# A transformer layer on one core: softmax sums divided through memory, bfloat16 transposes of the maxima, and filler products on TensorE

## The chip, the cores and the metric

One core of one Trainium2 chip runs the whole layer in one launch. The metric is the device time of one execution in microseconds; the median of several runs is compared. The engines are TensorE (PE, with its weight loads, PEld), VectorE (DVE), ScalarE (ACT), GpSimd (POOL) and SyncE (SP, which here only issues DMAs).

## The reference

The input x is 2 batches x 2048 tokens x 256 channels, float32. The layer is

```python
x = x + attention(layernorm(x))      # 16 heads of 16 channels, rotary q and k, causal
x = x + ffn(layernorm(x))            # 256 -> 704 -> 256, fp4-rounded inputs and weights
# attention, per head:
att = softmax(where(causal, q @ k.T / 4, -inf))
y = att @ v;  return y @ Wo.T + bo
# ffn:
h = silu(fp4(x) @ fp4(w_gate).T) * (fp4(x) @ fp4(w_up).T);  return fp4(h) @ fp4(w_down).T
```

fp4 rounds blocks of 16 channels to eight magnitudes after scaling by the block's largest value, so that earlier results must be nearly exact in float32.

## The kernel before

The tokens are cut into 8 chunks (b, c) of 512, four for each batch, and the 16 heads into 4 groups g of four. A pair (chunk, group) is a slot; there are 32. Work on a slot falls into four steps.

- **Maxima** (`max_steps`): for 128 queries at a time, TensorE computes scores with queries on partitions (line 1020, tile `sc`, two heads at once in two 64-row strips, causal mask added by line 988), and DVE reduces each 512-wide bank to a maximum (line 1044).
- **Turning the maxima**: DVE splits each maximum into three summands that fit bfloat16 (lines 1082 and 1085) and puts them into `mslots`, a float32 tile of 128 queries x 4 x (4 heads x 32 places). Four float32 transposes on TensorE (line 1098, tile `ptm`) put the queries on the free axis, and ACT casts them to the bfloat16 tile `mT` (line 1104).
- **Values** (`value_steps`): scores come again with keys on partitions (line 1158, tile `sx`), after a bfloat16 product that subtracts the maxima (line 1150, `less` x `mT`). ACT takes the exponential (line 1173), and TensorE multiplies by v (line 1206, tile `av`). v has a column of ones ahead of each head's 16 channels, so `av` holds for each head, in 32 partitions, one row of sums and 16 rows of unnormalised values, 512 queries wide. ACT copies it to `avs` (line 1228).
- **Dividing** (`divide`): four float32 transposes on TensorE (line 1240, tile `pty`) put queries back on partitions; DVE takes the reciprocal of the sums (line 1250) and multiplies (line 1254) into `y`, queries x channels.

When all four groups of a chunk are divided, `ffn_steps` runs for each of its four 128-token tiles: `y` is transposed once more, two float32 transposes (line 1296, `pth<-ident,y`) and an ACT copy to `yT` (line 1300, in the buffers `xT`), because the output product `po` (line 1380) needs channels on partitions; then come layernorm, fp4 rounding (mostly on POOL), the gate and up products `pg` (line 1430), their gating, rounding, and the down product `pd` (line 1523). Projections of the next chunk (`pj`, line 763, `pv`, line 945) run among them; their rotated q and k go to DRAM (`parts`, line 855) and come back in the strip layout (`qT`, line 866, and `kT`, line 879), all on SP's queue.

**What sets the order.** Every piece of work is a task with an engine, a cost in microseconds, a due time and the things it reads and writes. `Plan.ordered` simulates the engines with these costs, picks the task that can start first (among those within `PATIENCE` of the first, the one due earliest), gives buffers out as `ROOM` allows, and the instructions are emitted in that order. For the engines in `ORDERED` (PE, DVE, ACT, POOL) each instruction is chained to the one before it, so that the order stays; SP's DMAs are not chained, and may be moved ahead by the scheduler below. All engines run their instructions in order: an instruction that waits holds up those behind it.

The due times come from the slots: slot n's maxima, then slot n's values during slot n+1, the division after that (`divided`), and the FFN of a chunk spread over the slots after its last division. The last chunk's FFN has nothing to run beside, and uses its own due times and buffers (`last`).

Of the kernel before, what the change touches and what calls it, by code (L numbers as in the profile page):

```python
# [34 lines left out]
ALU = mybir.AluOpType  # L35
# [21 lines left out]
    mybir.EngineType.DVE,  # L57
    mybir.EngineType.Activation,
    mybir.EngineType.Pool,
)  # L60
MAGIC = 1.5 * 2.0**22
EXPONENT = 0x7F800000
# [5 lines left out]
CHANGE = 0.07  # L68
FEED_M = 0.0
FEED_V = 0.0  # L70
PATIENCE = 0.03
TURN = 0.4
ISSUE = 0.46

ON_VECTOR = (0, 1, 2, 3)
LAST = 0.05
# [6 lines left out]


XIN = 3
ROOM = dict(ps=7, av=1, ex=4, qT=5, parts=4)
ROOM.update(mx=2, mparts=1, left=1, mT=2, avs=1, den=2, y=2)
ROOM.update(xnT=1, xin=XIN, high=1, t1=1, t2=1, cs=1, dev=XIN-1)
ROOM.update(x0=1, xT=2, x1=2, xn=2, h=1, hrT=1, step=1, fdev=2, sc16=2, sc44=2)


ANY_TURN = ("ps",)
# [25 lines left out]


class Task:  # L120
    __slots__ = "engine cost run due tiling late left ready end after new kinds".split()


class Plan:
# [47 lines left out]
    def ordered(self):  # L172

        waiting = {e: [] for e in HOP}
        for n, t in enumerate(self.tasks):
            if not t.left:
                waiting[t.engine].append((t.due, n, t))
        number = {t: n for n, t in enumerate(self.tasks)}
        free = dict.fromkeys(HOP, 0.0)
        rooms = {kind: [] for kind in ROOM}  # L180
        turn = dict.fromkeys(ROOM, 0)
        tiling = "whole"
        dues = sorted(((t.due, n) for n, t in enumerate(self.tasks)), reverse=True)
        done = set()
        out = []

        def vacancy(kind, n, to):

            held = rooms[kind]
            n -= ROOM[kind] - len(held)  # L190
            if n <= 0:
                return 0.0, []
            some = []
            for thing in held:
                if all(u.end is not None for u in thing.users):
                    at = max(
                        u.end + (u.late if u.engine != SP else 0.0) + HOP[u.engine][to]
                        for u in thing.users
                    )
                    some.append((at, thing.number, thing))  # L200
            if len(some) < n:
                return None
            some = sorted(some)[:n]
            return some[-1][0], [thing for *_, thing in some]

        while len(out) < len(self.tasks):
            while dues and dues[-1][1] in done:
                dues.pop()
            horizon = dues[-1][0] + AHEAD
            choice = None  # L210
            for e, queue in waiting.items():
                queue.sort(key=lambda x: x[:2])
                able = []
                vacant = {}
                for due, n, t in queue:
                    if due > horizon or len(able) > 30:
                        break
                    at = max(t.ready, free[e])
                    for kind, some in t.kinds.items():
# [24 lines left out]
            e = t.engine  # L244
            waiting[e].remove((due, n, t))
            for kind, some in t.kinds.items():
                for thing in vacancy(kind, len(some), e)[1]:
                    rooms[kind].remove(thing)
                rooms[kind] += some
                turn[kind] += len(some)  # L250
            if e == PE:
                if t.tiling != tiling:
                    at += ENTER[t.tiling]
                tiling = t.tiling
            if e == SP:
# [12 lines left out]
        self.span = max(t.end for t in out)  # L268
        return out
# [29 lines left out]
def layer_kernel(  # L299
# [28 lines left out]


    const = ctx.enter_context(tc.tile_pool(name="const", bufs=1))  # L330
    qry = ctx.enter_context(tc.tile_pool(name="qry", bufs=5))
    spill = ctx.enter_context(
        tc.tile_pool(name="spill", bufs=4, space=bass.MemoryType.DRAM)
    )
# [52 lines left out]
        less.append(t)  # L387
    minus_half = const.tile([P, 1], F32, name="minus_half")
    nc.gpsimd.memset(minus_half, -0.5)
    mslots = const.tile([P, TPC, GROUP, SLOT], F32, name="mslots")  # L390
    nc.gpsimd.memset(mslots, 0.0)

# [592 lines left out]
    def masked(sc, h, col, mask):  # L985
        for half in range(2):
# [6 lines left out]
                stop=(half == 1),  # L993
            )

    maxima, max_ = {}, {}

    m_order, e_order = Thing(), Thing()
# [3 lines left out]
    def max_steps(b, c, g):  # L1002
# [89 lines left out]
        def turn(due):  # L1092
            pm = Thing("ps")

            def run():
                st["pt"] = small(CH, "ptm").rearrange("p (i q) -> p i q", i=TPC)
                for i in range(TPC):
                    nc.tensor.transpose(
                        st["pt"][:, i, :], mslots[:, i].rearrange("p s d -> p (s d)"), ident
                    )  # L1100

            def put():
                mT = att.tile([P, CH], BF16, tag="mT", name="mT")
                nc.scalar.copy(mT, st["pt"].rearrange("p i q -> p (i q)"))
                maxima[b, c, g] = mT

            add(
                PE,
                turning(TPC),
                run,  # L1110
                [slots_of, fixed],
                [pm],
                due - 0.1,
                [max_[b, c, g]],
                late=0.05,
            )
            add(ACT, on_scalar(CH), put, [pm], [max_[b, c, g]], due - 0.1)
# [5 lines left out]
        return steps, split, turn  # L1123

    rows, rows_ = {}, {}

    def value_steps(b, c, g):

# [96 lines left out]
        def close(due):  # L1225
# [3 lines left out]

            add(ACT, on_scalar(CH), run, [av_], [avs_], due)  # L1230

        def divide(due):
            pm = Thing("ps")
            if g == 0:
                rows_[b, c] = Thing("y")
# [80 lines left out]
    def ffn_steps(b, c, i, last=False):  # L1316
# [40 lines left out]
        def turn_attended(due):  # L1357
            def put():
# [8 lines left out]
                [things["x0"]],  # L1367
                due,
            )
            transposed(  # L1370
                lambda: rows[b, c][:, i, :], E, rows_[b, c], put, things["yT"], due
            )

        def attended(due):
            pm = Thing("ps")

            def run():
                po = st["po"] = small(E, "po")
# [10 lines left out]
                token("x1")  # L1389
                nc.vector.tensor_tensor(st["x1"], st["po"], st["x0"], ALU.add)  # L1390

            add(PE, KE * product(E), run, [things["yT"], wo_], [pm], due, [things["x1"]])
# [170 lines left out]
        ]  # L1563


    order = [(b, c) for b in range(B) for c in range(NC)]
    slots = NG * len(order)

    def placed(steps, lo, hi):
# [100 lines left out]
    for n in range(4):  # L1670

        to = spread[:, n, :].rearrange("p (h half x e) -> p h half x e", h=2, half=2, x=2)
        for twice in range(2):
            dst = to[:, :, twice, n % 2, :] if n < 2 else to[:, :, n % 2, twice, :]
            nc.vector.tensor_copy(dst, fold.rearrange("p (h e) -> p h e", h=2))
    begun = [(-10.0 + 0.01 * n, step) for n, (_, step) in enumerate(norm_steps(*order[0]))]
    steps = [step for _, step in project_steps(*order[0], 0)]
    raws = {}
# [113 lines left out]
```

## Time and profile before

| | |
|---|---|
| runs | 1398.01, 1398.54, 1400.73 us; median 1398.54 |
| profiled execution | 1400.22 us; its span, first to last instruction, is 1398.2 us |
| mean granted TensorE clock | 0.976 |
| DMA | 69.22 MB, mean 50 GB/s |
| SP | 426 DMA issues, 186.4 us of issuing |

The profile lists for each engine its busy time, then the same in 40 slices of 35 us as tenths. A group of instructions is shown as line, engine, operation, output<-inputs, shape and count, busy time and the mean ns of one, and then the idle time of its engine just before it with what ended that idle time. The matrix products in float32 stand as two records each; the transposes as one. The granted clock (PEclk) is the share of its full rate that TensorE was given.

### The profile page before, as it was taken

Reading aid. Unit: us, or ns where it says so; the run is one execution under the profiler, and the core shown is the slowest. Engines: PE = TensorE matmul, PEld = TensorE weight load, DVE = VectorE, ACT = ScalarE, POOL = GpSimd, SP = SyncE. Lnnn points to the kernel's source line nnn. Section 1 sums busy time; section 2 is a strip of 40 time slices with the busy share of each in tenths; the row PEclk is TensorE's granted clock in tenths of the full one; section 3 lists DMA queues with packets and bytes.
Section 4 is the critical chain, followed back from the end, with each engine's and each line's share of the span. In section 5 each row is a group of like instructions: output and inputs, shape, how many; then the busy total and the mean of one; then the engine's idle time right before and its main releaser. Section 6 shows DMA issues by size and latency. Waiting matters only on the chain. (4 is left out here: it accounts for less than half of the span.)

```text
span 1398.2 us, 27614 instructions
## 1 busy us (share of the span) xinstructions
PE 1338.2 (96%) x10437; PEld 675.2 (48%) x10437; DVE 1117.2 (80%) x2442; ACT 759.6 (54%) x1698; POOL 520.7 (37%) x671
## 2 busy tenths in 40 slices
PE   6898999999999999999999999999999999999986
PEld 3454445544544444444465455455454444444454
DVE  6779989988889988875477978998888988983286
ACT  2533665466556556567743455455655556667711
POOL 4655634434413433224353543242442331320342
PEclk9887999999999999999999999999999999999998
DMA  2443424202111301020422404130120120000000
GB/s 91 116 108 80 90 67 93 54 16 61 35 24 53 65 24 41 16 53 25 95 66 53 125 25 90 50 69 12 54 54 5 53 56 11 9 8 9 5 5 15
DMA packets 46316, 69.22 MB, mean 50 GB/s; under 512 B 6372, under 2 KB 22120, under 8 KB 46184
## 3 DMA queue, kind: packets, MB, share of 16 engines
q1 hardware_dynamic: 45888, 67.20, 20.4%
q8 instruction: 82, 1.34, 0.4%
q14 instruction: 50, 0.41, 0.1%
q10 hardware_dynamic: 296, 0.26, 0.1%
HBM read 47.52 MB, written 19.92 MB: 48 GB/s over the span
## 5 line engine op out<-in xcount | busy, mean ns | idle before, releaser
L1173 ACT ACTIVATE ex<-sx 128x512 f32<-128x512 f32 (+3 forms) x1280 | 594.0, 538 | 358.4 <-PE sx L1158 201.5
L1044 DVE TENSOR_REDUCE parts<-sc 128x1 f32<-128x512 f32 (+3 forms) x1152 | 638.9, 612 | 64.0 <-PE sc L1020 41.2
L1158 PE MATMUL sx<-qT,kT 64*128 64x512 f32 (+3 forms) x1280 | 339.2, 521 | 0.0
L1206 PE MATMUL av<-ex,v 128*32 128x512 f32 (+3 forms) x2560 | 300.6, 540 | 0.2 <-ACT ex L1173 0.2
L1020 PE MATMUL sc<-kT,qT 64*128 64x512 f32 (+3 forms) x1280 | 291.2, 430 | 9.1 <-DVE parts L1044 1.9
L1150 PE MATMUL sx<-mT,less 64*128 64x512 bf16 (+3 forms) x1280 | 249.5, 355 | 4.7 <-DVE mx L1044 2.0
L1020 PEld LDWEIGHTS sc<-kT,qT 64*128 64x128 f32 x1280 | 138.5, 190 | 156.9 <-DVE parts L1044 46.8
L517 POOL TENSOR_SCALAR inv<-inv 128x16 f32<-128x16 f32 (+2 forms) x82 | 18.0, 220 | 509.7 <-DVE inv L513 472.0
L1150 PEld LDWEIGHTS <-less 64*128 64x128 bf16 x1280 | 68.6, 94 | 211.1 <-issue 203.5
L1158 PEld LDWEIGHTS sx<-qT,kT 64*128 64x128 f32 x1280 | 132.6, 195 | 8.9 <-issue 6.5
L1523 PE MATMUL pd<-wdT,hrT 128*128 128x256 f32 (+1 forms) x384 | 103.6, 410 | 0.7 <-ACT hrT L1300 0.3
L1206 PEld LDWEIGHTS av<-ex,v 128*32 128x32 f32 x2560 | 52.0, 108 | 74.2 <-issue 65.9
L1523 PEld LDWEIGHTS pd<-wdT,hrT 128*128 128x128 f32 (+1 forms) x384 | 70.0, 197 | 29.8 <-issue 15.6
L1430 PE MATMUL pg<-wgT,xT 128*128 128x352 f32 x224 | 77.1, 478 | 1.0 <-ACT qb L776 0.3
L1044 DVE TENSOR_REDUCE mx<-sc 128x1 f32<-128x128 f32 (+3 forms) x128 | 54.6, 479 | 25.8 <-PE sc L988 25.6
L1430 PE MATMUL pg<-wuT,xT 128*128 128x352 f32 x224 | 74.3, 472 | 0.2
L763 PE MATMUL pj<-xnT,wqkT 128*128 128x512 f32 x128 | 73.3, 671 | 1.1 <-DVE v L954 0.6
L542 POOL TENSOR_TENSOR h<-h,step 128x704 f32<-128x704 f32 x28 | 47.2, 1686 | 68.6 <-DVE step L539 66.9
L988 PE MATMUL sc<-pick,mask_q 64*128 64x64 bf16 x1024 | 70.9, 201 | 0.0
L1456 ACT ACTIVATE h<-pg 128x352 f32<-128x352 f32 x64 | 30.0, 469 | 69.2 <-PE pg L1430 59.6
L815 POOL TENSOR_TENSOR t<-t,cs 128x512 f32<-128x512 f32 x31 | 39.6, 1279 | 75.1 <-DVE t L809 70.5
L988 PE MATMUL sx<-pick,mask_k 64*128 64x64 bf16 x1024 | 64.1, 196 | 0.0
(153 smaller groups left out, 1592.1 us busy)
## 6 DMA issues: line engine op xcount, KB each, us to landing
qT<-parts SPq DMA_DIRECT2D x120, 128.0 KB
kT<-parts SPq DMA_DIRECT2D x120, 128.0 KB
parts<-high SPq DMA_DIRECT2D x30, 256.0 KB
parts<-t SPq DMA_DIRECT2D x30, 256.0 KB
cs<-in_rope_dram SPq DMA_DIRECT2D x8, 512.0 KB
xin<-in_L_attn_x_dram SPq DMA_DIRECT2D x28, 128.0 KB
x<-in_L_attn_x_dram SPq DMA_DIRECT2D x28, 128.0 KB
out_dram<-x SPq DMA_DIRECT2D x28, 128.0 KB
```

The lines of the kernel that those rows point to most:

```text
L542: queue.tensor_tensor(src(), src(), st["step"], ALU.add)
L763: nc.tensor.matmul(got["pj"], lhsT=wqkT[:, k, i, cols], rhs=xnTs[b, c][:, k, :], start=(k == 0), stop=(k == KE - 1),)
L815: (nc.gpsimd if early and i == 0 else queue).tensor_tensor(swapped, swapped, angles[b, c][:, 1, :], ALU.mult)
L988: nc.tensor.matmul(sc[h][:, col + at : col + at + STRIP], lhsT=strips(mask, h, half), rhs=strips(pick, h), start=False, stop=(half == 1),)
L1020: nc.tensor.matmul(sc[h][:, :cols], lhsT=strips(qT, h, d, slice(i * P, (i + 1) * P)), rhs=strips(kT, h, duo, slice(0, cols)), start=True, ...
L1044: nc.vector.tensor_reduce(dst, got[0][h][:, :cols], AX.X, ALU.max)
L1150: nc.tensor.matmul(sc[h][:, off:], lhsT=strips(less[d], h), rhs=strips(mT, h, slice(off, CH)), start=True, stop=False,)
L1158: nc.tensor.matmul(sc[h][:, off:], lhsT=strips(kT, h, duo, slice(jj, jj + P)), rhs=strips(qT, h, d, slice(off, CH)), start=False, stop=(j ...
L1173: nc.scalar.activation(st[j, d][:, h, off:], got[0][h][:, off:], AF.Exp, scale=HD**-0.5)
L1206: nc.tensor.matmul(st["av"][SLOT * s : SLOT * (s + 1), off:], lhsT=v[:, at : at + SLOT], rhs=st[j, d][:, h, off:], start=(j == 0), stop=(j ...
L1430: nc.tensor.matmul(got[half], lhsT=split("xrT")[:, k, :], rhs=wT[:, k, half * IH : (half + 1) * IH], start=(k == 0), stop=(k == KE - 1),)
L1523: nc.tensor.matmul(st["pd"], lhsT=st["hrT"][:n, k, :], rhs=wdT[:n, k, :], start=(k == 0), stop=(k == KI - 1),)
```

## The change

1. **Division** (all chunks but the last; the last keeps the old path). `laid_apart` writes `avs` to DRAM (`sums`), reads the 4 x 512 sums back as a 128 x 16 tile (`den`), takes the reciprocal there on DVE, writes it to DRAM, and reads it back with each row repeated over 16 partitions (`over`). The 64 rows of values are read from DRAM into `y`, which now has channels on partitions. After each second group POOL multiplies 128 x 512 by `over`. There are five DMAs for each group. `po` takes `y` directly as its stationary operand; the transpose to `yT` and its copy go.
2. **Maxima**: the four transposes of line 1098 read the upper halves of `mslots` as bfloat16, with a bfloat16 identity, into a bfloat16 bank.
3. **Filler products**: between a task due at -999 and one due at 12 (`KEPT`), `keep` puts products of the identity with its first 64 columns, whose result nothing reads, into TensorE's order ahead of each task whose planned idle time is over 0.1 us, one for each 0.12 us. In the built program there are 268, of which 46 stand ahead of the first projection.
4. **Order and buffers**: SP joins `ORDERED`; `PATIENCE` goes from 0.03 to 0.06; the `qT` buffers go from 5 to 4 and `xT` from 2 to 1.

```diff
+    mybir.EngineType.SP,
...
-PATIENCE = 0.03
+PATIENCE = 0.06
...
+KEPT = 12.0
+SPARED = 0.1
...
-ROOM = dict(ps=7, av=1, ex=4, qT=5, parts=4)
-ROOM.update(mx=2, mparts=1, left=1, mT=2, avs=1, den=2, y=2)
+ROOM = dict(ps=7, av=1, ex=4, qT=4, parts=4)
+ROOM.update(mx=2, mparts=1, left=1, mT=2, avs=1, den=2, y=2, sums=2, over=1)
...
-ROOM.update(x0=1, xT=2, x1=2, xn=2, h=1, hrT=1, step=1, fdev=2, sc16=2, sc44=2)
+ROOM.update(x0=1, xT=1, x1=2, xn=2, h=1, hrT=1, step=1, fdev=2, sc16=2, sc44=2)
...
             def run():
-                st["pt"] = small(CH, "ptm").rearrange("p (i q) -> p i q", i=TPC)
+                upper = mslots.bitcast(BF16).rearrange("p i s (d two) -> p i (s d) two", two=2)
+                bank = ps_s.tile([P, TPC, P], BF16, tag="ps", name="ptm")
+                st["pt"] = bank
                 for i in range(TPC):
-                    nc.tensor.transpose(
-                        st["pt"][:, i, :], mslots[:, i].rearrange("p s d -> p (s d)"), ident
-                    )
+                    nc.tensor.transpose(st["pt"][:, i, :], upper[:, i, :, 1], ident_b)
...
-                turning(TPC),
+                0.01 + 0.08 * TPC,
...
+        def laid_apart(due):
...
+            def out():
+                st["sums"] = spill.tile([P + GROUP, CH], F32, tag="sums", name="sums", bufs=2)
+                nc.sync.dma_start(st["sums"][:P], st["avs"])
+            def dens():
+                st["den"] = att.tile([P, HD], F32, tag="den", name="den")
+                nc.sync.dma_start(
+                    st["den"], inner()[:, 0, :].rearrange("s (n e) -> s n e", e=HD)
+                )
+            def over_out():
+                nc.sync.dma_start(
+                    st["sums"][P:].rearrange("s (n e) -> s n e", e=HD), st["den"]
+                )
+            def sums():
...
+                nc.sync.dma_start(rows[b, c][at, g // 2, :], inner()[:, 1:AUG, :])
+            def over_in():
...
+                nc.sync.dma_start(
+                    overs[b, c][at],
+                    st["sums"][P:].unsqueeze(1).to_broadcast([GROUP, HD, CH]),
+                )
+            def times():
+                y = rows[b, c][:, g // 2, :]
+                nc.gpsimd.tensor_tensor(y, y, overs[b, c], ALU.mult)
+            add(SP, landing(256), out, [avs_], [sums_], due)
+            add(SP, landing(8) , dens, [sums_], [den_], due)
+            add(SP, landing(128), sums, [sums_], [y_part], due, [rows_[b, c]])
+            add(DVE, 0.25, lambda: nc.vector.reciprocal(st["den"], st["den"]), [], [den_], due)
+            add(SP, landing(8), over_out, [den_], [sums_], due)
+            add(SP, landing(128), over_in, [sums_], [over_part], due, [over])
...
+            if g % 2:
...
+                add(POOL, on_pool(CH), times, [*over.parts, *pair], [*pair, rows_[b, c]], due)
         def divide(due):
+            if (b, c) != order[-1]:
+                return laid_apart(due)
...
-            transposed(
-                lambda: rows[b, c][:, i, :], E, rows_[b, c], put, things["yT"], due
-            )
+            if last:
+                transposed(
+                    lambda: rows[b, c][:, i, :], E, rows_[b, c], put, things["yT"], due
+                )
...
-                        lhsT=split("yT")[:, k, :],
+                        lhsT=(
+                            split("yT")[:, k, :]
+                            if last
+                            else rows[b, c][:, k, i * P : (i + 1) * P]
+                        ),
...
+    def keep(n=1):
+        if not kept:
+            kept.append(small(P, "kept"))
+        for _ in range(n):
+            nc.tensor.matmul(
+                kept[0][:, :STRIP], lhsT=ident, rhs=ident[:, :STRIP], start=True, stop=True
+            )
+    add(PE, 0.3, keep, [fixed], [held], -999.0)
+    add(PE, 0.3, keep, [held], [], KEPT)
...
     for t in plan.ordered():
+        if t.engine == PE and held.users[0].end <= t.start <= held.users[-1].end:
+            keep(max(0, int((t.idle - SPARED) / 0.12)))
         t.run()
```

More of the change, by code (lines that the diff above doesn't have):

```diff
@@ L120 @@
 class Task:
-    __slots__ = "engine cost run due tiling late left ready end after new kinds".split()
+    __slots__ = "engine cost run due tiling late left ready end after new kinds start idle".split()
 class Plan:
@@ L254, in ordered @@
                 tiling = t.tiling
+                t.start, t.idle = at, at - free[e]
             if e == SP:
@@ L330, in layer_kernel @@
     const = ctx.enter_context(tc.tile_pool(name="const", bufs=1))
-    qry = ctx.enter_context(tc.tile_pool(name="qry", bufs=5))
+    qry = ctx.enter_context(tc.tile_pool(name="qry", bufs=4))
     spill = ctx.enter_context(
@@ L389, in layer_kernel @@
     nc.gpsimd.memset(minus_half, -0.5)
+    ident_b = const.tile([P, P], BF16, name="ident_b")
+    nc.vector.tensor_copy(ident_b, ident)
     mslots = const.tile([P, TPC, GROUP, SLOT], F32, name="mslots")
@@ L994, in masked @@
             )
+    order = [(b, c) for b in range(B) for c in range(NC)]
     maxima, max_ = {}, {}
@@ L1125, in layer_kernel @@
     rows, rows_ = {}, {}
+    overs, over_ = {}, {}
     def value_steps(b, c, g):
@@ L1230, in close, with inner @@
             add(ACT, on_scalar(CH), run, [av_], [avs_], due)
+        def laid_apart(due):
+            if g == 0:
+                rows_[b, c] = Thing("y")
+            if g % 2 == 0:
+                over_[b, c, g] = Thing("over")
+            over = over_[b, c, g - g % 2]
+            wide = GROUP * HD
+            at = slice(g % 2 * wide, g % 2 * wide + wide)
+            sums_, den_ = Thing("sums"), Thing("den")
+            y_part, over_part = Thing(of=rows_[b, c]), Thing(of=over)
+            rows_[b, c].parts = getattr(rows_[b, c], "parts", []) + [y_part]
+            def out():
+                st["sums"] = spill.tile([P + GROUP, CH], F32, tag="sums", name="sums", bufs=2)
+                nc.sync.dma_start(st["sums"][:P], st["avs"])
+            def inner():
+                return st["sums"][:P].rearrange("(s r) q -> s r q", s=GROUP)
+            def dens():
[8 more added lines that the diff above has]
+            def sums():
+                if g == 0:
+                    rows[b, c] = att.tile([P, KE, CH], F32, tag="y", name="y")
+                nc.sync.dma_start(rows[b, c][at, g // 2, :], inner()[:, 1:AUG, :])
+            def over_in():
+                if g % 2 == 0:
+                    overs[b, c] = att.tile([P, CH], F32, tag="over", name="over", bufs=1)
+                nc.sync.dma_start(
[11 more added lines that the diff above has]
+            add(SP, landing(128), over_in, [sums_], [over_part], due, [over])
+            over.parts = getattr(over, "parts", []) + [over_part]
+            if g % 2:
+                pair = rows_[b, c].parts[-2:]
+                add(POOL, on_pool(CH), times, [*over.parts, *pair], [*pair, rows_[b, c]], due)
@@ L1390, in put @@
                 nc.vector.tensor_tensor(st["x1"], st["po"], st["x0"], ALU.add)
-            add(PE, KE * product(E), run, [things["yT"], wo_], [pm], due, [things["x1"]])
+            turned = things["yT"] if last else rows_[b, c]
+            add(PE, KE * product(E), run, [turned, wo_], [pm], due, [things["x1"]])
             add(DVE, on_vector(E), put, [pm, things["x0"]], [things["x1"]], due)
@@ L1563, in ffn_steps @@
         ]
-    order = [(b, c) for b in range(B) for c in range(NC)]
     slots = NG * len(order)
@@ L1675, in layer_kernel @@
             nc.vector.tensor_copy(dst, fold.rearrange("p (h e) -> p h e", h=2))
+    held = Thing("ps")
+    kept = []
+    def keep(n=1):
[7 more added lines that the diff above has]
+    add(PE, 0.3, keep, [held], [], KEPT)
     begun = [(-10.0 + 0.01 * n, step) for n, (_, step) in enumerate(norm_steps(*order[0]))]
```

## The prediction, made before the changed kernel ran

> **What bounds the kernel now.** I read the busy times first, then the 40 slices, then the busy times by stage, and last the order of time around one removed transpose.
>
> ```profile
> PE 1338.2 (96%) x10437; PEld 675.2 (48%) x10437; DVE 1117.2 (80%) x2442; ACT 759.6 (54%) x1698; POOL 520.7 (37%) x671
> PE   6898999999999999999999999999999999999986
> DVE  6779989988889988875477978998888988983286
> PEclk9887999999999999999999999999999999999998
> ```
>
> PE is busy nearly throughout; only the first five slices (to 175 us) and the last two show gaps. The granted clock is low in just these places. A busy PE could still be a waiting PE, since ends are modelled. So I took the distance from the start of each group of products to the start of the next, between 175 and 1330 us: 214 value products of 512 columns take 0.996 us at the 10th and 0.999 at the 90th percentile, and with every group put at the median of its kind the sum is 97% of the time that passed. PE runs at its own rate there, and what leaves it there comes off the time.
>
> ```profile
> core 0: us, PE busy (x) PEld busy (x) DVE busy (x) ACT busy (x) POOL busy (x), PEclk, DMA share, GB/s
> 29.20:39.50 10.30, 10.02 (x54) 5.11 (x56) 8.44 (x25) 2.90 (x6) 3.73 (x7) 0.50 0.01 2
> 42.90:49.70 6.80, 5.81 (x44) 3.94 (x44) 6.59 (x23) 3.51 (x7) 4.41 (x8) 0.50 0.27 77
> 80.40:94.10 13.70, 13.41 (x84) 7.36 (x82) 11.55 (x33) 2.23 (x5) 4.94 (x7) 0.50 0.40 112
> 124.80:141.90 17.10, 14.05 (x64) 8.00 (x62) 16.69 (x45) 3.87 (x8) 7.59 (x12) 0.50 0.11 29
> 175.00:1330.00 1155.00, 1138.15 (x9128) 560.87 (x9121) 925.22 (x1978) 677.62 (x1496) 400.89 (x473) 1.00 0.19 45
> ```
>
> The first four rows are the stretches between 29 and 142 us where the clock is a half. DVE is busy for 43.3 of their 47.9 us. In the last row PE idles for 16.9 us and DVE is busy for 80%.
>
> **Division, on TensorE.** The next view gives the price.
>
> ```profile
> 860.96 0.59 PE L1158 MATMUL sx<-qT,kT 64*128 64x512 f32 x2
> 861.49 0.66 PE L1240 MATMUL pty<-ident,avs 128*128 128x128 f32 x4
> 861.98 0.38 PE L1296 MATMUL pth<-ident,y 128*128 128x128 f32 x2
> 862.20 1.02 PE L763 MATMUL pj<-xnT,wqkT 128*128 128x512 f32 x2
> ```
>
> The columns are start, length over all, and the group. From start to next start the four transposes of `avs` hold PE for 0.49 us (mean of the 27 such groups after 175 us: 0.517), the two of `y` for 0.22 here (mean of 28: 0.43, since others wait for the shape to change). Seven of eight chunks leave both: 28 groups x 0.517 = **14.5 us**, and 28 tiles x 0.43 = **12.0 us**. The way in counts too: from the score product at 860.96 to the transposes are 0.53 us, where one score pair follows another after 0.457 (median). 56 insertions x 0.07 = 4 us; with zero and twice that as ends I take **4**.
>
> **Division, elsewhere.** These rows leave with them.
>
> ```profile
> L1250 DVE RECIPROCAL den<-pty 128x16 f32<-128x16 f32 x32 | 7.8, 245 | 7.8 <-PE pty L1240 7.8
> L1254 DVE TENSOR_TENSOR y<-pty,den 128x256 f32<-128x256 f32 x32 | 13.6, 425 | 1.1
> L1300 ACT COPY xT<-pth 128x256 f32<-128x256 f32 x56 | 21.2, 388 | 10.1 <-PE pth L1296 10.0
> ```
>
> DVE loses 28 x 0.425 = 11.9 us (the reciprocal stays, on the same 128x16), ACT 28 x 0.388 = 10.9. POOL gains 14 products of 128x512 at 1.279 (row `t<-t,cs`), 17.9 us on an engine busy for 37%. Hidden behind PE, all of it, and counted at nothing; without that cover POOL's 1.28 would stand once in each chunk's chain.
>
> SP gains 140 issues: 28 x (0.58 for 256 KB, as `parts`, and 4 x 0.35, as the loads of x) = 55 us on 186 of issuing. It also waits, and what it waits for shows in its own waits:
>
> ```profile
> SPq L866 <- DMA parts<-t: 46.8, 14, 4.2
> SPq L879 <- DMA parts<-t: 18.8, 14, 2.6
> ```
>
> Total, times, longest. A trip to DRAM and back makes SP wait 1.3 to 3.3 us on average, 4.2 at most. The chain from `avs` to a divided `y` is 0.59 (copy), 2.0 of issues, four landings of 2.1 to 4.2, 0.25 (reciprocal) and 1.28 (POOL): 12 to 21 us in place of some 1.3. Behind its waiting DMAs in SP's queue stand q and k for later slots, x for the FFN, and stores. The chain costs PE something only if `po` comes up in PE's order before it is done. In the changed program's order, priced with the distances above, PE has 16 to 48 us of other work between the last value product of each of the seven chunks and its first `po`. The shortest, 16, belongs to chunk (0, 3). So one chunk may wait up to 5 us: I take **+2**, with 0 and 5 x 7 = 35 as ends.
>
> **Maxima.** 32 groups of four float32 transposes become bfloat16. No bfloat16 transpose is in the trace. The float32 one has a start-to-start of 109 ns; the upper bound is no gain. For bfloat16 the subtraction product (line 1150) averages 388 ns at 512 columns and 223 at 128: 0.43 ns a column, 55 ns for 128. 4 x 54 x 32 = **6.9 us** off; the ends are 0 and 14 (all of it, 32 x 0.44). I take 6.9, since the per-column rate is a bfloat16 row's own. If the two-byte reads at a stride of four bytes cost extra, the gain shrinks towards nothing.
>
> **Filler products and the clock.** 268 products of 64 columns in float32, two records each. A float32 record of 352 columns has a start-to-start of 296 ns (gate products), so 64 columns make 54 ns, and one filler 0.108: 29 us in all at full clock, twice that at half. PE idled 27 us before 175 us. Laid into waits the fillers cost nothing, laid over work 29. Their purpose can only be the clock. Had the half-rate stretches run at full rate, PE's 43.3 busy us there would be 21.6 less, but DVE, busy for 43.3 of the 47.9, would leave 4.6. I take **-5** for the clock (ends 0 and -21.6) and **+2** for fillers that miss a wait (ends 0 and 29).
>
> Here the trace and a rule part. In the half-rate stretches PE is busy for 43.3 of 47.9 us, and its longest wait between 20 and 175 us is this, after the last of them:
>
> ```profile
> PE ptm L1098 <- DVE x L1390: 2.5, 1, 2.5
> ```
>
> The Trainium skill, page "TensorE: Matmul & The Clock Gate", section "What's actually happening", has the clock fall to a half after an idle window of about 3.4 us. No such idle window is in that row, so the trace does not bear the rule out as it stands; something weaker than full idleness was enough. By the rule the fillers would cure nothing and the clock term would be 0, the time 5 us higher.
>
> **Order and buffers.** `PATIENCE` reshuffles the order: it can win at most the 16.9 us that PE idles after 175 us, and lose as much by the same measure; I take 0. One `qT` buffer less lets q for the next slots come later; zero in the sum, and a rival below. One `xT` less goes with `yT`, its second user. SP's chaining takes away early starts such as the x loads, which wait in SP's queue for up to 35.7 us (SP's waits, line 1353), so nothing is lost.
>
> **The sum**, on the profiled execution's 1400.22 us (span 1398.2 and 2.0 around it): -14.5 - 12.0 - 4 - 6.9 - 5 + 2 + 2 = -38.4, so 1361.8. The median of the runs shown is 1.7 lower than that execution; against it **1360 us**. Next bound: still PE after 175 us, with DVE at (925 - 12) of about 1120, 82%.
>
> **Rivals.**
>
> - *The clock comes back whole, and waits close too.* If DVE's load in the half-rate stretches moves under other work, the clock gives 21.6 rather than 5: 1360 - 16.6 = **1343**. For it: DVE has 22 us of idle time between 29 and 175 us. Against: in each stretch it is DVE that is nearly full.
> - *DVE becomes the bound.* DVE releases the banks of `sc`. In slices such as 910 to 945 it is busy for 34.3 of 35 us. If it sets the pace wherever PE is relieved, only its own loss counts, 11.9 us, with part of the clock: about **1383**. Against: the medians at 97%.
> - *Slower: q comes late.* With four `qT` buffers, the second pair of a block can be loaded only after an earlier slot's values are done, and in SP's queue it stands behind the division's landings; 9 of 15 block loads are split in two in the changed order. `sc` and `sx` of a slot stand at the head of PE's order and hold everything. It decides from 38 us over 28 slots: 1.4 us a slot. At 2 us, less than one landing, it gives 1360 + 56 = **1416**. For it: the waits on landings average 1.3 us and more. Against: slots last 13 to 71 us (from one turning of maxima to the next), and a buffer frees a slot ahead of its use.
> - *The change does not do what it says*: the clock stays at a half in the same places and fillers fall on work, +29 and the 5 lost: 1360 + 32 = **1392**, still within reach of the removed transposes.
>
> **How the numbers follow.** The sum 0.53, the whole clock 0.14, DVE 0.15, no use of the fillers 0.08 (half of it within 0.2% of before, which is 2.8 us and about what a measurement of this kernel can tell from no change), late q 0.10. Faster: 0.53 + 0.14 + 0.15 + 0.04 = 0.86; same 0.04; slower 0.10. The unknowns of the first case (transposes 0 to 14, way in 0 to 8, chain 0 to 35, PATIENCE) spread it by some 15 each way. The range runs from below the whole clock's 1343 to past DVE's 1383: 1336 to 1388, leaving out 0.18 above and a little below.
>
> **What would show it.** Right: `ptm` distances near 55 ns; no `pty` or `pth<-ident,y` before the last chunk; the stage from 175 us to the tail shorter by about 33 us with PE as busy; the clock at full from 20 to 175 us with at most 5 us won. Wrong: idle PE ahead of `po` released by POOL (the chain), ahead of `sc` or `sx` released by a DMA into `qT` (late q), bank waits on DVE in the steady stage, or half-rate stretches in the same places.

## The result and the profile after

| | before | after |
|---|---|---|
| median of 6 runs, us | 1399.08 | 1445.61 |
| lowest to highest | 1398.01 to 1402.88 | 1435.44 to 1457.19 |
| granted clock, by run | 0.976 (profiled) | 0.959 to 0.976 |

The change makes the kernel slower: ratio 1.0318, 95% interval 1.0275 to 1.036. I had said 1360 us. The profiled execution of after is its slowest run (1457.19 us, clock 0.959, so that its profile overstates the clock losses); it is not counted in the ratio, and where a time of after is compared below, it is the median of the other five, 1442.58 us. These five go from 1451.4 us at a granted clock of 0.966 to 1435.4 at 0.976, 16 us for 0.010 of the clock.

The same rows of the page, now of after: busy times, then the slices of PE, DVE and the clock.

```profile
PE 1403.8 (96%) x10805; PEld 734.7 (50%) x10805; DVE 1112.7 (76%) x2415; ACT 751.1 (52%) x1670; POOL 537.8 (37%) x685
...
PE   9999999999999999999998999999999999999986
...
DVE  5457698897888888888448978898888978894276
...
PEclk9589899999999999999999999999999999999998
```

PE is fuller than before in the first five slices and DVE emptier. The clock is low in the second slice, in the midst of filler products. From the costliest groups, the fillers and their weight loads:

```profile
L1760 PE MATMUL kept<-ident 128*128 128x64 f32 x536 | 89.6, 327 | 1.3 <-POOL ident masks.py:199 1.3
L1760 PEld LDWEIGHTS kept<-ident 128*128 128x128 f32 x536 | 82.9, 238 | 7.3 <-issue 4.3
```

They are busy for 90 us, where I had reckoned 29. The stages of after (start:end, length, busy us of PE, PEld, DVE, ACT and POOL with counts, clock, DMA share, GB/s):

```profile
32.00:73.00 41.00, 40.48 (x210) 29.06 (x210) 22.38 (x61) 8.03 (x17) 12.62 (x21) 0.50 0.17 43
175.00:1330.00 1155.00, 1128.61 (x8932) 554.33 (x8928) 948.66 (x2032) 648.91 (x1426) 429.46 (x513) 0.99 0.25 58
```

In the first row PE is busy for 40.48 of 41 us, and the clock is a half all through. I measured progress by the turning of the maxima (`ptm`), which happens once in a slot. Up to the eighth, after has fallen back from 229.2 us to 279.3, 50 us. From there to the 32nd it needs 1051.1 us against 1044.6, although 22 us of transposes have left TensorE in this stretch (`pty` 12.4 to 1.1 us and `pth<-ident,y` 10.4 to 0, both as start to next start) and the maxima's transposes hold it for 7.9 us instead of 13.4. So there are two losses to find: 50 us at the start, and a relief that did not show.

### The profile page after: what moved, and what is told of

It is laid out like the page before. It is cut to its first block, busy times and chain, and to the rows that moved or that the text cites. A ratio compares the mean times of both kernels' runs of the same rounds, so it can differ in the third digit from the quotient of the medians.

```text
span 1455.4 us, 28529 instructions
## 1 busy us (share of the span) xinstructions
PE 1403.8 (96%) x10805; PEld 734.7 (50%) x10805; DVE 1112.7 (76%) x2415; ACT 751.1 (52%) x1670; POOL 537.8 (37%) x685
## 4 chain that ended last, share of the span: by engine, by line
PE 67%; DVE 15%; DMA 7%; issue 5%; POOL 4%; ACT 1%; SPq 1%; POOLq 0%; DVEq 0%; ACTq 0%
PE av L1216 14%; PE sc L1028 10%; PE pg L1507 8%; PE sx L1160 8%; PE sx L1168 7%; DVE parts L1052 6%; PE pd L1600 5%; PE kept L1760 5%; PE pj L770 3%; PE pth L1367 2%; DMA kT<-parts 2%; PE po L1452 2%; DMA den<-sums 1%; PE pv L952 1%; PE sc L995 1%
## 5 line engine op out<-in xcount | busy, mean ns | idle before, releaser
L1216 PE MATMUL av<-ex,v 128*32 128x512 f32 (+3 forms) x2560 | 303.9, 547 | 0.0
L1028 PE MATMUL sc<-kT,qT 64*128 64x512 f32 (+3 forms) x1280 | 295.1, 433 | 9.1 <-ACT ex L1183 3.9
L1760 PE MATMUL kept<-ident 128*128 128x64 f32 x536 | 89.6, 327 | 1.3 <-POOL ident masks.py:199 1.3
L1760 PEld LDWEIGHTS kept<-ident 128*128 128x128 f32 x536 | 82.9, 238 | 7.3 <-issue 4.3
L1600 PEld LDWEIGHTS pd<-wdT,hrT 128*128 128x128 f32 (+1 forms) x384 | 70.3, 197 | 28.7 <-issue 16.4
```

Source lines behind the costliest of these rows:

```text
L1028: nc.tensor.matmul(sc[h][:, :cols], lhsT=strips(qT, h, d, slice(i * P, (i + 1) * P)), rhs=strips(kT, h, duo, slice(0, cols)), start=True, ...
L1216: nc.tensor.matmul(st["av"][SLOT * s : SLOT * (s + 1), off:], lhsT=v[:, at : at + SLOT], rhs=st[j, d][:, h, off:], start=(j == 0), stop=(j ...
L1600: nc.tensor.matmul(st["pd"], lhsT=st["hrT"][:n, k, :], rhs=wdT[:n, k, :], start=(k == 0), stop=(k == KI - 1),)
L1760: nc.tensor.matmul(kept[0][:, :STRIP], lhsT=ident, rhs=ident[:, :STRIP], start=True, stop=True)
```

## The experiments

Each time is a median with the ratio to the kernel before and its 95% interval. "Half-rate" is the time at a granted clock of a half in the one profiled execution, between 190 us and 80 us ahead of the end, read off the clock's records. A kernel's profile is one execution, and its clock can differ from that of the runs beside it.

**1. No fillers.** `kept` and its bank stay, the loop goes.

```diff
     for t in plan.ordered():
-        if t.engine == PE and held.users[0].end <= t.start <= held.users[-1].end:
-            keep(max(0, int((t.idle - SPARED) / 0.12)))
         t.run()
```

> The changed kernel with the loop that emits the filler products taken out; the plan, its order, the bank held for them and everything else stay. Theory A (the fillers are the loss): in the changed kernel's trace the 268 fillers hold TensorE for 86 us from start to next start, 0.32 us each where the plan reckons 0.12, and the kernel is 50 us behind the kernel before when the eighth slot's maxima are turned. Without them these 50 us go: 1390 to 1400 us, and the stage after stays level with before. Rival B (the division's landings and the new order are the loss, and the fillers lie in waits that stay): 1425 us or more, with TensorE idle where the fillers were.

1426.85 us, 1.0196 (1.0170 to 1.0222). 16 us better than after, neither theory's number. The fillers are a good part of the loss, not all of it.

**2. Fillers alone**, with their held bank, on the kernel before (every other part undone).

> The kernel before with the filler products alone: old division, old float32 maxima, old buffers, old PATIENCE, SP not chained. The plan now puts in 324 of them. Theory A: 324 x 0.32 = 104 us of TensorE, of which some 27 to 50 lie in waits, so 50 to 75 us slower than before: 1450 to 1475 us. Rival B: no more than 10 us slower, 1400 to 1410.

1427.14 us, 1.0203 (1.0188 to 1.0218): 28 us lost, between the two theories. The trace holds 502 records, so 251 fillers rather than the 324 I named. At the turning of the eighth slot's maxima it is 15.3 us behind before; from the eleventh on it stays 25.4 to 25.7 us behind. The half-rate time in the first 190 us falls from 47.8 to 13.7, and the loss is there all the same. Within a row of fillers the median distance from start to start is 0.112 us a record at full clock (0.213 at half, from after's trace), two records a filler, where I had put 0.054 a record.

**3. Division alone** (with its four `qT` and one `xT`; float32 maxima, no fillers, no held bank, old `PATIENCE`, SP not chained).

> The kernel before with the division through DRAM alone, with its buffers (four qT, one xT): float32 maxima, no fillers and no bank held, old PATIENCE, SP not chained. Theory C (the 27 us of transposes taken off TensorE are given back as waits of score products for banks and as short half-clock stretches, as the changed kernel's stage from the ninth slot's maxima to the last one's, 1051 us against 1045, suggests): 1385 to 1400 us. Rival D (the transposes are worth what they held, and it was the other parts of the change that took it back): 1365 to 1375 us.

1439.67 us, 1.0291 (1.0275 to 1.0307): worse than either theory, 41 us lost by the part that was to take 26 us off TensorE. First come waits of PE and SP's wait for a buffer of x, then what SP did, all of this kernel; the middle number is the count, the last the longest wait.

```profile
PE po L1450 <- POOL y L1286: 6.4, 2, 4.2
PE pth L1365 <- POOL xn L552: 5.7, 1, 5.7
```

```profile
SPq L680 <- PE ptx L698: 14.3, 1, 14.3
```

```profile
495.26 0.34 SPq L1267 DMA_DIRECT2D sums<-den  x1
510.21 0.35 SPq L680 DMA_DIRECT2D xin<-in_L_attn_x_dram  x1
510.65 0.54 SPq L1279 DMA_DIRECT2D over<-sums  x1
```

The last three are neighbours in SP's queue. A load of x stands ahead of the reciprocals' way back; it waits 14.3 us for its buffer, and `over`, `y` and then `po` wait with it. `po` starts at 515.59 us after 4.25 us of waiting, and from 514.5 us the clock is a half for 13.7 us.

**4. Fillers in bfloat16**, 256 columns in one record each, in the changed kernel.

```diff
-            kept.append(small(P, "kept"))
+            kept.append(small(2 * P, "kept"))
...
-                kept[0][:, :STRIP], lhsT=ident, rhs=ident[:, :STRIP], start=True, stop=True
+                kept[0],
+                lhsT=ident_b,
+                rhs=mask_q.rearrange("p a b -> p (a b)"),
+                start=True,
+                stop=True,
```

> The changed kernel with the same 268 filler products at the same places, each now one bfloat16 product of the bfloat16 identity with 256 columns of a mask (result not read) in place of the float32 one of 64 columns. Theory A (a float32 filler costs three times its planned price because two weight loads of 128 columns go with two passes of 64): each holds TensorE for about 0.12 to 0.15 us, 32 to 40 us in all, mostly in waits: 1390 to 1405 us; and if denser streaming is what keeps the clock up, the half-rate stretch from 32 to 73 us goes too. Rival B: 1430 us or more, and the half-rate stretches stay.

1423.49 us, 1.0184 (1.0164 to 1.0204): 19 us below after, with the same count at the same places, and between the two theories. A filler is now one record of 0.109 us from start to start (median), about the planned price. The half-rate time in the first 190 us is 13.7 us instead of the 64.9 without fillers; the time gained over no fillers is 3.4 us, with intervals that overlap, so it is not clear of noise.

**5. No fillers and no held bank.** The two `add(PE, 0.3, keep, ...)` lines go too.

> The changed kernel without the filler products and without the two tasks that hold a PSUM bank for them until the due time 12; the rest of the change stays, and the plan is made anew with seven banks in the first slots. Theory E (the held bank costs in the first slots, where score banks are short): the first eight slots take 10 to 18 us less than in the run without fillers, so 1408 to 1417 us. Rival F (the first slots are slow since the division's landings and the half clock hold them): 1423 to 1430 us, as without fillers.

1415.61 us, 1.0131 (1.0112 to 1.0151). The bank held until due time 12 cost 11 us, as theory E had it; the plan is made anew with the seventh bank, so its new order is part of these 11 us.

**6. TensorE relieved, nothing in its place.** Same plan and order as before; one of four transposes of `avs`, one of two of `y`.

```diff
-                for i in range(TPC):
+                for i in range(1):
                     nc.tensor.transpose(
                         pt[:, i].rearrange("p s d -> p (s d)"),
...
-            for k in range(full + (rest > 0)):
+            for k in range(1 if one else full + (rest > 0)):
```

> The kernel before, same plan and same order, with TensorE relieved and nothing put in its place: of the four transposes of avs one is made and DVE reads its result four times, of the two transposes of y one is made and ACT copies it twice. So the attention result is wrong in most tokens, and 128 of 192 transposes at 109 ns are left out: 14 us of TensorE. Theory G (the steady stage goes at TensorE's own rate; the changed kernel lost its gain to its new order and its chain): 1383 to 1388 us. Rival C (relief is given back as waits for banks): 1393 to 1399 us.

1399.11 us over 10 runs, 0.9999 (0.9988 to 1.0011). 128 transposes of 109 ns, 14 us of TensorE, are gone, and nothing is gained. 21 of the 31 slots have the length they had to within 0.3 us. This is the plainest answer to the prediction: what leaves TensorE does not come off the time. The half-rate time is 13.7 us, against 3.4 before.

**7 and 8. DVE relieved**, in the kernel before and in the one of experiment 5: of each bank off the diagonal only half goes into the maximum. The order stays.

```diff
-                nc.vector.tensor_reduce(dst, got[0][h][:, :cols], AX.X, ALU.max)
+                nc.vector.tensor_reduce(
+                    dst, got[0][h][:, : CH // 2 if kc < c else cols], AX.X, ALU.max
+                )
```

> The kernel before with DVE relieved: of the 512 columns of each score bank off the diagonal only the first 256 go into the maximum (768 reductions take about half their 0.68 us, some 250 us of DVE less; the maximum subtracted is then one over part of the keys, so the exponentials are scaled otherwise). Theory C (banks are freed late by DVE and ACT, and that sets part of the pace): 20 us or more faster than before, 1379 us or less. Theory G (TensorE's own rate): within 10 us of before, 1389 to 1399.

> The changed kernel without fillers and held bank, with DVE relieved in the same way (256 of 512 columns in the maximum off the diagonal). Theory C: the relief of TensorE comes to light when DVE no longer holds the banks: 30 us or more below the same kernel with full maxima, and 20 us or more below the kernel before with light maxima. Theory G with the chain and order as the loss: no more than 10 us below the same kernel with full maxima, and slower than the kernel before with light maxima.

1377.04 us, 0.9846 (0.9830 to 0.9863), and 1389.96 us, 0.9941 (0.9926 to 0.9956). DVE, 80% busy, was part of the bound: 22 us and 26 us come off. But with the relief the changed kernel still trails by 13 us, where theory C had it 20 us or more ahead, so theory C alone does not explain it here.

**9. Transposes made twice**, same order as before.

```diff
-                for i in range(TPC):
+                for i in (*range(TPC), *range(TPC)):
...
-            for k in range(full + (rest > 0)):
+            for k in (*range(full + (rest > 0)), *range(full if twice else 0)):
```

> The kernel before, same plan and order, with each of the transposes of avs and of y on TensorE made twice into the same bank: 192 transposes at 109 ns more, 21 us of TensorE. Theory G (TensorE's own rate sets the pace): 1418 to 1422 us. Theory C (these transposes stand where TensorE would wait for a bank anyhow, as the relieved kernel's unchanged time suggests): 1400 to 1408 us.

1408.91 us, 1.0074 (1.0057 to 1.0090): 10 us for 21 us of work, between the two theories. There is no half-rate time in the stage.

**10. The chain cut.** The kernel of experiment 5; POOL multiplies by `bvb`, the bias of v that is there from the start, instead of `overs`.

> The changed kernel without fillers and held bank, same order, where POOL's product no longer multiplies by the returned reciprocals but by the bias of v, which is there from the start; the attention result is wrong. All five DMAs and the reciprocal still run, but y is ready when its own DMAs have landed. In the last groups of the chunks the chain measured 14 to 23 us (38 in the first chunk) from avs to y, where 12 to 21 were reckoned. Theory H (late chains make TensorE wait at po and drop its clock): 1400 to 1408 us. Rival I (the wait at po is one of 2.5 us; the loss is in waits for banks and their clock drops all over the stage): 1411 to 1418 us.

1409.32 us, 1.0081 (1.0066 to 1.0096). The wait for the returned reciprocals costs 6 us, a little less than theory H had; the half-rate time is 23.9 us instead of 51.2. The other 10 us above the next experiment are not waits for the returned reciprocals.

**11 and 12. All but division and fillers; bfloat16 maxima alone** (both with four `qT` and the two `xT` of before).

> The kernel before with everything of the change but the division, the fillers and the smaller xT: bfloat16 maxima, four qT buffers, PATIENCE 0.06, SP chained. Theory J (the division's DMAs, POOL products and places in the order cost the 16 us that the changed kernel without fillers and bank is slower): 1392 to 1402 us. Rival K (PATIENCE, SP's chaining and the fewer q buffers spoil the order by themselves): 1410 us or more.

> The kernel before with the bfloat16 maxima alone, and four qT buffers (the bfloat16 identity leaves no room for five). 32 groups of four transposes now hold TensorE for 0.33 us in place of 0.56, 7 us less. Theory C (relief is given back): 1396 to 1403 us. Theory G: 1390 to 1393 us.

1398.77 us, 1.0003 (0.9994 to 1.0013), and 1402.85 us, 1.0027 (1.0003 to 1.0051). `PATIENCE`, SP's chaining and one `qT` less, taken together with the cheaper maxima, cost nothing that can be told, and the cheaper maxima bring nothing.

**13. Maxima's transposes three times**, in the kernel of experiment 5.

> The changed kernel without fillers and held bank, same order, with the bfloat16 transposes of the maxima made three times into the same bank: 256 more, about 57 ns each, 15 us of TensorE. Theory L (work put on or taken off TensorE is mostly taken back by its clock: in the profiles so far the half-rate time between 190 us and the tail is 0 with transposes doubled, 3.4 us before, 13.7 relieved, 51.2 in this kernel): 1412 to 1421 us and a mean granted clock above this kernel's 0.957. Rival G (TensorE's work counts in full): 1428 to 1432 us at the same clock.

1420.47 us, 1.0162 (1.0136 to 1.0189); the granted clock of its runs is 0.960 to 0.966, of experiment 5's 0.954 to 0.959. 5 us for 15 us of work, as theory L expected, though the interval overlaps experiment 5's; the 15 us in full, rival G's number, are excluded.

**14 to 16. Half the scores.** The maximum off the diagonal over half the keys, with the products of the other half left out too, in the kernel before, in that of experiment 11, and in that of experiment 5.

```diff
-            cols = CH if kc < c else (i + 1) * P
+            cols = CH // 2 if kc < c else (i + 1) * P
```

> The kernel before where the maximum off the diagonal is taken over half the keys, and the score products of the other half are left out as well (the softmax is the same as long as no exponential overflows, since any shift does). The plan knows it. DVE loses some 250 us, TensorE 384 pairs at about 0.1 us, 38 us. Theory C (DVE, by way of the banks, sets the pace together with TensorE): well below the 1377 us of DVE's relief alone, 1340 to 1362 us. Rival L (what leaves TensorE is taken back by the clock): 1368 to 1378 us.

> The same half maxima on the kernel with all of the change but division and fillers (bfloat16 maxima, four qT buffers, PATIENCE 0.06, SP chained). Theory C: with DVE out of the way, TensorE's 7 us show: 4 to 10 us below the kernel before with half scores. Theory L: within 4 us of it.

> The same half maxima on the changed kernel without fillers and held bank, so with the division through DRAM. Theory C: TensorE's 33 us show at least in part, and it is 10 us or more below the kernel before with half scores. Theory L with the chain: as fast or slower than that, by up to 20 us, with a lower granted clock.

1369.58 us, 0.9803 (0.9786 to 0.9821); 1358.16, 0.9711 (0.9692 to 0.9731); 1353.02, 0.9671 (0.9632 to 0.9710). Experiment 14 falls in theory L's range and misses theory C's: the score products left out make it only 7 us faster than experiment 7, which relieves DVE alone, although they held TensorE for 32 us (202 to 170 us, start to next start). Against 14 the parts of the change now pay, 11 us by the smaller ones and 17 us with the division too; the division's own 5 us are not clear of noise, since the last two intervals overlap. The last has the lowest median of all, below both kernels. It holds only where no exponential overflows, since a key left out of the maximum may exceed it. DVE in the middle of the run, first of 14 and then of 16:

```profile
190.00:1270.00 1080.00, 1055.80 (x8756) 543.12 (x8756) 728.51 (x1934) 647.01 (x1434) 391.42 (x459) 1.00 0.20 46
```

```profile
190.00:1270.00 1080.00, 1051.50 (x8696) 533.27 (x8696) 727.97 (x1914) 645.47 (x1422) 407.62 (x473) 0.99 0.24 58
```

DVE is busy for 67%, where it was 81% in the kernel before (909.72 of 1120 us from 190 us on).

**17 and 18. Division alone, with SP chained, and with the new `PATIENCE`.** One line each, against experiment 3.

> The division alone (old PATIENCE, float32 maxima, no fillers, no bank) with SP chained. In the division alone POOL waited up to 20 us for a DMA into over, and one chain took 34 us at a chunk's end. Theory M (SP's free order let other DMAs ahead of the chain's): 1440 falls to 1415 to 1425 us. Rival N (the order made with PATIENCE 0.03 is what costs): 1435 us or more.

> The division alone with PATIENCE 0.06 in place of 0.03, SP not chained. Theory M: 1432 us or more. Rival N: 1415 to 1425 us.

1418.03 us, 1.0138 (1.0119 to 1.0157), and 1440.29, 1.0294 (1.0275 to 1.0313). SP's order makes 22 us, `PATIENCE` nothing. POOL's waits for `over`, first unchained, then chained:

```profile
POOL y L1286 <- DMA over<-sums: 53.0, 10, 20.4
```

```profile
POOL y L1287 <- DMA over<-sums: 30.7, 9, 11.5
```

## Why the prediction was wrong, by its own steps

The runs part the loss of 43.5 us (1442.58 against 1399.08): fillers 16 us, their bank 11, division 17 (experiment 5 against 11), the other parts 1. These are steps from one kernel to the next, so they add up by construction; and only the first keeps the order, as the plan is made anew in the others.

- **"What leaves it there comes off the time"** is the step that failed, and 37 us of the sum hung on it. I took steady distances for TensorE's own rate, but a distance that repeats can hold a wait that repeats. In the same order, transposes taken away give 0 of 14 us (experiment 6), and doubled they cost 10 of 21 (9). The distances from start to next start show the same: with three of four transposes of `avs` left out, their groups fall from 17.4 to 10.4 us in all, but with one of two of `y` left out, theirs stay at 12.1 for 12.4 us, so the product behind them starts no sooner. My 12.0 us for `y` held waits that stay. With DVE relieved in the plan too (14 to 16) the kernels with the change are faster than the one without, but not by a price of the transposes: the plans differ, and the division's share is not clear of noise.

  What holds TensorE instead is in part DVE, which must empty the banks of scores: DVE's relief alone, in the same order, takes 22 us off (7). Waits of PE's weight loads for a bank of scores were in the trace of before, from 190 to 1310 us; the columns are the total, the count and the longest:

```profile
PEld sc L1020 <- DVE parts L1044: 41.2, 71, 0.8
...
PEld sc L1020 <- ACT ex L1173: 25.6, 45, 0.8
```

The same two rows of experiment 6, same stretch, and then of experiment 5, from 190 to 1325 us, where TensorE has less to do:

```profile
PEld sc L1020 <- DVE parts L1044: 41.5, 72, 0.9
PEld sc L1020 <- ACT ex L1173: 28.4, 49, 0.8
```

```profile
PEld sc L1028 <- DVE parts L1052: 44.5, 71, 2.1
PEld sc L1028 <- ACT ex L1183: 42.5, 73, 1.2
```

They grow from 67 to 70 and 87 us. That the freed time has become waits for the readers of the scores is how I read it, and is not shown: weight loads run beside products, and experiment 11, level with before, has 78 us of these waits. The rival "DVE becomes the bound" had the engine right; DVE was part of the bound already, beside TensorE, and the price of 1383 us was too mild.
- **The clock takes some of it back**, and the sum had no term for that. Between 190 us and the tail the half-rate time is 0 us with transposes doubled, 3.4 before, 13.7 relieved, 51.2 in experiment 5; in the same four, PE idles for 14.8, 16.4, 20.0 and 27.6 us from 190 us to between 1310 and 1325. Idle time alone does not settle it: experiment 11 has 20.5 us of half rate with 15.5 us idle. I had priced a wait by its length, but the clock can fall with it: in experiment 5 a wait of 2.45 us at `po` ends at 725.07 us, and 1.5 us later a stretch of 3.4 us at half begins. Its rows are these, with start and length ahead and the wait in the brackets:

```profile
722.02 0.59 PE L1452 MATMUL po<-woT,y 128*128 128x256 f32 x2
...
725.07 0.70 PE L1452 MATMUL po<-woT,y 128*128 128x256 f32 x2 [2.45 <-POOL y L1288]
```

How much of a loss the clock can be is estimated from the granted clocks of all runs: the span times the missing share is the clock lost, and its direct cost is at most that. Averaged over the runs it is 36 us before and 39 relieved, measured side by side, so of experiment 6's 14 us the clock can hold about 3. It is 40 us in experiment 11, 54 in 10 and 61 in 5. From 11 to 5 that is 21 us more, or 18 against the kernel before of each session, and the division loses 17: there the clock could be all of the net loss. How much of it is clock and how much is banks I could not part.
- **Fillers, "+2, ends 0 and 29"**: mis-sized. I scaled a 352-column record by its columns to 0.054 us, but start to start is 0.112, about the 109 ns of a float32 transpose, which has the same weights and twice the columns. That row was before me. Fillers and the waits behind them hold TensorE for 86 us in after (groups from start to next start), and 16 us of it was time. The rival "the change does not do what it says" had this right in kind: fillers fell on work, and the clock stayed at a half from 32 to 73 us.
- **The held bank** was no term at all: `Thing("ps")` takes one of seven banks for the first slots, and giving it back gains 11 us. I read the products and not what they reserve.
- **The clock term, -5**: neither borne out nor refuted. With fillers of the planned price (4 against 1) 51 us of half rate go from the first 190 us, and the time falls by 3.4, which is not clear of noise and has the fillers' own cost in it. In after itself the first 190 us have 64.9 us at half, as many as without fillers, and 41 of them lie among the fillers.
- **The chain, "+2"**: in experiment 5, 14 to 23 us from the end of the copy to `avs` to the end of the product into `y` in every second group (32 to 38 in the first chunk), where I reckoned 12 to 21, and one wait of 2.45 us at `po`, where I said up to 5 us at one chunk. Cutting it gives 6.3 us. The mechanism was right, the size too low. SP's chaining, which I had at nothing, keeps the cost as low as it is: without it the division loses 22 us more.
- **Maxima, -6.9**: right on the engine, 0.33 us a group for 0.56, and 56 ns from start to start where I had estimated 55; worth nothing in time (experiment 12).
- **q comes late**, the one rival on the slower side: its cause was not seen. Experiment 11, with four `qT`, is level with before, so the time went that way for other reasons.

The division's remaining 10 us (experiment 10 against 11) stay open. The chain's DMAs, POOL's products and the order of a new plan were not tried apart, and the clock lost differs by 13 us between the two kernels.

## What to carry to other kernels

Before an engine's freed time is counted as a gain, free it: leave the work out in the same order and look. An engine that is busy for 96% may still move in part at another's pace, by way of the buffers that the other must release, and steady distances don't tell the two apart. A filler's price is its measured distance from start to start, not its columns, and the buffer it reserves comes on top. A chain of DMAs needs its place in the queue kept.

## What the runs showed of the hardware

- A granted clock of a half lasted for 41 us in after while the records had TensorE busy for 99%, 17 us of it with float32 products of 64 columns; so the records' busy share does not tell what clock will be granted. 256-column bfloat16 fillers at the same places left 13.7 us of half rate in the first 190 (experiment 4).
- The length of a wait does not tell it either. Stretches of half rate began within 1.6 us of the end of waits of 2.35, 2.45 and 2.85 us (at `po` and at a transpose of `h`, in experiments 1 and 5). But a longer wait at a transpose of `h`, in experiment 4, was followed by none until 476 us, and the stretch that began at 479.8 us in experiment 1 had no wait of PE over 0.4 us in the 7 us ahead of it. The wait of experiment 4 and the clock behind it:

```profile
231.94 0.87 PE L1367 MATMUL pth<-ident,h 128*128 128x128 f32 x6 [3.30 <-POOL h L555]
...
231.90:240.00 8.10, 8.06 (x87) 5.35 (x87) 3.83 (x10) 3.65 (x12) 6.43 (x7) 1.00 0.05 6
```

- A float32 product of 64 columns takes as long from start to start as a float32 transpose of 128, 0.112 against 0.109 us, each with weights of 128 x 128; the bfloat16 transpose of 128 takes 0.056.
